# Second LayerNorm's turned tokens: stored from 128 partitions at a time, loaded back 32 partitions at a time

## The chip, the cores and the metric

One core of one Trainium2 chip. The metric is the device time of one execution in microseconds (us), lower is better; the time before is the median of three runs. A profiled execution gives, beside its own time, the span from the first to the last instruction of the program and the trace that the views below are taken from.

## The reference, cut to what matters

The input `x` has 2 batches of 2048 tokens of 512 features, in float32. A condition vector gives, through one matrix, six rows per batch (shift, scale and gate, twice).

```python
emb = dot(silu(t), ada_w) + ada_b            # six parts of 512
norm  = ln(x) * (1 + scale_msa) + shift_msa
h     = gelu(dot(norm, ssm_w1) + ssm_b1)
x     = x + gate_msa * (dot(h, ssm_w2) + ssm_b2)
norm2 = ln(x) * (1 + scale_mlp) + shift_mlp  # the second LayerNorm
hf    = gelu_tanh(dot(norm2, ff_w1) + ff_b1)
x     = x + gate_mlp * (dot(hf, ff_w2) + ff_b2)
```

## The kernel before

**Blocks.** The 4096 tokens are cut into eight blocks of 512 (`NBLK` = 8). A first part of the kernel runs `norm1(i)`, `ssm1(i)` and `ssm2(i)` for each block: the first LayerNorm and the two small products. Behind `ssm2(i)` comes `norm2(i)`, the second LayerNorm, whose result is kept in DRAM. A second part runs four steps `s` over pairs of blocks: `ff1(s)` for the pair, then `ff2(s, 0)` and `ff2(s, 1)`. The matrix products are cut by Winograd's variant of Strassen's scheme, so sums and differences of operands (lines 256 and 283) run on VectorE, GpSimd and ScalarE beside TensorE.

**Turning the tokens.** A product needs features on the partitions, LayerNorm has tokens there. `normed` (statistics, scales, then for each of four groups `c` of tokens a normalization on ScalarE and a transpose on VectorE, `turn`, line 591) does this in squares of 32 by 32. What comes out, the block `bl`, has partition `a*32 + q`, where `a` numbers a group of 32 partitions, and columns `(m, r)` with `m` of 4 and `r` of 512. The product needs it with `a` and `m` exchanged: partition `m*32 + q`, columns `(a, r)`. A DMA makes this exchange. There are three ways in the kernel:

- `move`: 16 DMAs of 64 KB from SBUF to SBUF, 32 partitions to 32 partitions. Only `norm1(2)` uses it.
- `turned_out`: four DMAs of 256 KB to DRAM, one for each `a`, each reading 32 partitions of `bl`, 8 KB from each, and writing pieces of 2 KB to the places where they belong in a DRAM tensor that has the wanted order. `norm1(3)` to `norm1(7)` use it, and one DMA of 1 MB (8 KB for each of 128 partitions) loads the whole block back. 
- `norm2(i)` uses the same `turned_out` for all eight blocks (`SOON` holds all of them). The blocks come back much later, in `normed2(i)` (called by `tokens(s)`, which `ff1(s)` calls): four DMAs of 256 KB, one for each `a`, each writing 2 KB to all 128 partitions.

After the loads `modulate` (ScalarE, line 274) applies scale and shift in place, one instruction for each of four feature groups `k`. Each reads all partitions and all `a`, so it needs all four loads. The pair's two token tiles `turned2[0]` and `turned2[1]` lie where the tokens of `norm1` lay before (`turned_r`): block 0 of the second part takes the place of `turned[6]`, block 1 that of `turned[7]`.

**Order.** `Plan` records every operation with a cost and the cells that it reads and writes, and `order()` simulates the engines to put all operations in one order. Each engine, and SyncE (SP) for nearly all DMAs, then runs its own in that order. A DMA's planned cost depends on its bytes. All DMAs are issued by line 316, all `tensor_tensor` work by line 256, all ScalarE activations by line 274, copies by line 283, matmuls by line 294. DMAs of SP rotate through eight semaphores; a DMA that takes a semaphore waits until the eighth DMA before it has landed.

**A reader's names.** In the views `far`, `ring`, `rows`, `near`, `hidden`, `fw` and `turned` are SBUF regions; `turned<-far` is a store of a turned block (norm1 and norm2 alike: `bl` lies in `far`, and the DRAM tensors too are called turned), `turned<-turned` a load back from DRAM.

Of the kernel before, what the change touches and what calls it, by code (L numbers as in the profile page):

```python
# [198 lines left out]
def kernel(  # L199
# [17 lines left out]
    P = 128  # L217
    B, N, D = x.shape
    H = fw1.shape[1]
    KD, KH = D // P, H // P  # L220
    C = 4
# [4 lines left out]
    G = 32  # L226
    SOON = tuple(range(NBLK))
# [14 lines left out]
    def cols(ap):  # L242
        n = 1
        for d in ap.shape[1:]:
            n *= d
        return n
# [64 lines left out]
    def dma(o, a, q="s", lead=0.0, lat=2000.0, sooner=0.0):  # L311
        size = max(cols(o.unsqueeze(0)), 1) * 4
        outs = [o] if o.tensor.name in scratch else []
        ins = [a] if a.tensor.name in scratch else []
        lead = lead or (0.0 if ins or not outs or size <= plan.LITTLE else 25000.0)
        plan.add(q, lambda E: E.dma_start(out=o, in_=a), outs, ins, {q: plan.ISSUE}, {q: lat}, size=size, lead=lead)  # L316
        plan.ops[-1].sooner = sooner
# [19 lines left out]
    def far(name, *shape):  # L337
        t = dram.tile(list(shape), F32, tag=name, name=name)
        scratch.add(t.tensor.name)
        return t  # L340

    def kb(t, at, n):
        return t[:, at * 256 : (at + n) * 256]

    def cut(t, form, **sizes):
        return t.rearrange(form, **sizes)
# [6 lines left out]
    for n in range(8):  # L353
        t = psum.tile([P, 2 * HT], F32, tag=f"bank{n}", name=f"bank{n}")
# [5 lines left out]

    x1_d = [far(f"x1_{i}", P, C, D) for i in range(NBLK)]
    turned1_d = {i: far(f"turned1_{i}", P, C, D) for i in range(3, NBLK)}
    turned_d = {i: far(f"turned_{i}", P, C, D) for i in SOON}
    fw1_d = far("fw1_parts", 7, P, 7, W)
    fw2_d = far("fw2_gated", P, KH, D)
    fw2_sd = far("fw2_sums", P, 3, KH // 2, D // 2)
# [4 lines left out]
    xs = [cut(slots[i % 5], "p (c d) -> p c d", c=C) for i in range(NBLK)]  # L371
# [15 lines left out]
    passing = (kb(near_r, 24, 2), kb(hidden_r, 30, 2))  # L387
# [128 lines left out]
    def stats(xt, slots=range(C)):  # L516
        t = marks[norms[0] % 4]
        norms[0] += 1
        mv = cut(t[:, :8], "p (c two) -> p c two", c=C)
        for c in slots:  # L520
            st, src, dst = t[:, 8 + 6 * c : 14 + 6 * c], xt[:, c, :], mv[:, c, :]
            plan.add("v", lambda E, st=st, src=src: E.bn_stats(st, src), [st], [src], {"v": 694}, {"v": 680})  # L522
            plan.add("v", lambda E, st=st, dst=dst: E.bn_aggr(dst, st), [dst], [st], {"v": 100}, {"v": 182})
        return t, mv

    STATS_BY_ACT = (2, 4, 5)
# [13 lines left out]
    def stats_by_act(xt, unread):  # L540

        t, mv = stats(xt, ())
        less, half = t[:, 52:56], D**-0.5
        for c in range(C):
            act_sum(unread, xt[:, c, :], AF.Identity, mv[:, c, :1], 0.0, 1.0 / D)
        small("g", lambda E: E.tensor_scalar(less, mv[:, :, 0], -half, None, ALU.mult), less, [mv[:, :, 0]])
        for c in range(C):
            act_sum(unread, xt[:, c, :], AF.Square, mv[:, c, 1:], less[:, c : c + 1], half)
        return t, mv

    def scales(t, mv, v="g", slots=slice(0, C)):
        full = [t[:, 32 + C * n : 32 + C * (n + 1)] for n in range(5)]
        ve, r, e, rstd, nmr = [a[:, slots] for a in full]
        var, mean, half = mv[:, slots, 1], mv[:, slots, 0], half_t[:, slots]
        small("g", lambda E: E.tensor_scalar(ve, var, 1.0, EPS, ALU.mult, ALU.add), ve, [var])
        small("g", lambda E: E.tensor_tensor(r, ve, half, ALU.pow), r, [ve, half], 1090)
        if v == "v":
            small(v, lambda E: E.tensor_tensor(e, r, ve, ALU.mult), e, [r, ve])
            small(v, lambda E: E.scalar_tensor_tensor(e, e, -0.5, r, ALU.mult, ALU.mult), e, [e, r])
            small(v, lambda E: E.scalar_tensor_tensor(rstd, e, 1.5, r, ALU.add, ALU.mult), rstd, [e, r])  # L560
            small(v, lambda E: E.scalar_tensor_tensor(nmr, mean, -1.0, rstd, ALU.mult, ALU.mult), nmr, [mean, rstd])
        else:
            small(v, lambda E: E.tensor_tensor(e, r, r, ALU.mult), e, [r])
            small(v, lambda E: E.tensor_tensor(e, e, ve, ALU.mult), e, [e, ve])
            small(v, lambda E: E.tensor_scalar(e, e, -0.5, 1.5, ALU.mult, ALU.add), e, [e])
            small(v, lambda E: E.tensor_tensor(rstd, r, e, ALU.mult), rstd, [r, e])
            small(v, lambda E: E.tensor_tensor(nmr, mean, rstd, ALU.mult), nmr, [mean, rstd])
            small(v, lambda E: E.tensor_scalar(nmr, nmr, -1.0, None, ALU.mult), nmr, [nmr])
        return full[3], full[4]
# [4 lines left out]
    def normal(o, xt, c, rstd, nmr, e="a"):  # L574
        dst, src, b, s = slot(o, c), xt[:, c, :], nmr[:, c : c + 1], rstd[:, c : c + 1]
        if e == "a":
            act(dst, src, AF.Identity, b, s)
        else:
            plan.add(
                "v",  # L580
                lambda E: E.tensor_scalar(dst, src, s, b, ALU.mult, ALU.add),
                [dst],
                [src, b, s],
                {"v": 560},
                {"v": 640},
            )

    def turn(bl, src, c):
        o = cut(bl, "p (m k c q) -> p k m c q", m=C, k=KD, c=C)[:, :, :, c, :]
        a = cut(slot(src, c), "p (k m q) -> p k m q", k=KD, m=C)  # L590
        plan.add("v", lambda E: E.transpose(o, a), [o], [a], {"v": 636}, {"v": 705})  # L591

    def modulate(t, k, which, b):
        o = t[:, :, k * P : (k + 1) * P]
        act(o, o, AF.Identity, mods[which][:, k, b : b + 1], mods[which + 1][:, k, b : b + 1])
# [3 lines left out]
    def next_blocks():  # L599
        turns[0] += 1  # L600
        return blocks[turns[0] % 2]
# [9 lines left out]
    def normed(src, dst, bl, by_act=False):  # L611
        t, mv = stats_by_act(src, banks[2]) if by_act else stats(src)
        rstd, nmr = scales(t, mv)
        for c in range(C):
            normal(dst, src, c, rstd, nmr)
            turn(bl, dst, c)
        return cut(bl, "p (m r) -> p m r", m=C)

    def move(to, bl, queues="s"):
        for a in range(C):  # L620
            for m in range(C):
                q = queues[m % len(queues)]
                dma(to[m * G : (m + 1) * G, a, :], bl[a * G : (a + 1) * G, m, :], q, lat=2000.0 + 16 * plan.ISSUE / len(queues))

    def turned_out(to, bl):
        for a in range(C):
            dma(to[:, a].rearrange("(m q) r -> q m r", m=C), bl[a * G : (a + 1) * G])
# [50 lines left out]

    def norm2(i):
        plan.stage = f"norm2 {i}"  # L680
        turned_out(turned_d[i], normed(xs[i], passing if i else xs[i], next_blocks(), i in STATS_BY_ACT))

# [317 lines left out]
    def normed2(i):  # L1002
        plan.stage = f"tokens {i}"
        t = turned2[i % 2]
        if i in SOON:
            for a in range(C):
                dma(t[:, a], turned_d[i][:, a])
        else:
            dma(t, x1_d[i])
            move(t, normed(t, t, kb(far_r, 0, 8)))  # L1010
        for k in range(KD):
            modulate(t, k, 3, i // PER_B)

    def tokens(s):
        plan.stage = f"tokens {s}"
        q = {}
        for n in range(2):
            i = 2 * s + n
            if i in SOON:
                normed2(i)  # L1020
            q[f"1{n + 1}"], q[f"2{n + 1}"] = turned2[n][:, :, :W], turned2[n][:, :, W:]
        return second(q, thirds(outer_s), cuts=2)
# [381 lines left out]
    modulation(3, 1)  # L1404
    plan.care = 0.3
    norm2(0)
    load_ada(5)
    modulation(4, 2)
# [8 lines left out]
    for i in range(1, NBLK):  # L1417
        if i + 3 < NBLK:
            plan.care = 0.2
            tok[i + 3] = norm1(i + 3)  # L1420
            plan.care = 0.45
        last = i + 2 >= NBLK
        hooks = second_head(i + 1, hid[i + 1]) if last and i + 1 < NBLK else {}
        ssm2(i, hid[i], w2_ops, CARRIED, hooks)
        if i in SOON:
            norm2(i)
        if i == 4:
            ff = weight_fw2(0, 1)
            fw2_sixth(*ff)
        if i + 1 == PER_B:  # L1430
            w2_ops = weight2(1, 1)
            quarter_row(1)
            w2_leaves[0] = second_leaves(w2_ops)
        if not last:
            hid[i + 2] = ssm1(i + 2, tok[i + 2], w1_ops, second_head(i + 1, hid[i + 1]))
# [62 lines left out]
```

## Time and profile before

| what | value |
|---|---|
| median of three runs | 568.1 us (567.44 to 570.17) |
| profiled execution, its own time | 569.21 us |
| its span, first to last instruction | 567.4 us |
| granted TensorE clock | 0.999 |
| moved by DMA | 119.85 MB, mean 211 GB/s |

The span is what the views divide up; 1.8 us of the profiled execution's own time lie outside it. PE is TensorE's matmuls, PEld its weight loads, DVE VectorE, ACT ScalarE, POOL GpSimd, SPq the issues on SyncE's queue. In the timeline a row merges neighbours of one kind: start, duration from the first start to the last end, and the count.

### The profile page before, as it was taken

The page shows a single profiled execution, that of the slowest core. Times are in us where ns is not written, and L with a number is a line of the kernel's source. Part 1 is how long each engine was busy: PE and PEld are TensorE (multiplying, and loading weights), DVE is VectorE, ACT ScalarE, POOL GpSimd, SP SyncE. Part 2 cuts the span into 40 slices and gives each one's busy share as a digit, 9 for nine tenths or more (in the row PEclk, how much of TensorE's full clock was granted, in tenths as well). Part 3 has the DMA queues.
Part 4 walks back from the last instruction along what each step waited for, and adds up shares of the span by engine and source line. Part 5 has one row for each costly group of instructions (what it writes and reads, how often), then busy time and mean ns, then how long its engine had stood idle before and what let it go on. Part 6 is the DMA issues. An engine that isn't in the chain of part 4 may idle for free.

```text
span 567.4 us, 10428 instructions
## 1 busy us (share of the span) xinstructions
PE 559.0 (99%) x3577; PEld 506.5 (89%) x3577; DVE 489.0 (86%) x918; ACT 271.8 (48%) x558; POOL 384.1 (68%) x523
## 2 busy tenths in 40 slices
PE   8999999899999999999999999999999999999997
PEld 4888889788897988889999889999889999888997
DVE  5696988799886988989989889999999898789785
ACT  3464856777685875659112356222266222335120
POOL 2887547598934598994767897667795685446660
PEclk9999999999999999999999999999999999999999
DMA  8954899987899867896054889168955041820022
GB/s 314 399 217 90 246 360 277 320 299 264 258 310 307 270 217 220 276 317 217 20 186 152 304 279 342 68 205 274 319 174 207 2 150 43 273 93 29 1 75 74
DMA packets 53057, 119.85 MB, mean 211 GB/s; under 512 B 5473, under 2 KB 10509, under 8 KB 51470
## 3 DMA queue, kind: packets, MB, share of 16 engines
q1 hardware_dynamic: 51842, 118.66, 62.6%
q8 instruction: 28, 0.46, 0.4%
q10 hardware_dynamic: 1164, 0.55, 0.3%
q14 instruction: 23, 0.19, 0.1%
HBM read 77.63 MB, written 40.51 MB: 208 GB/s over the span
## 4 chain that ended last, share of the span: by engine, by line
PE 89%; DMA 6%; DVE 2%; ACT 1%; SPq 1%; issue 0%; DVEq 0%; ACTq 0%
PE bank L294 89%; DMA turned<-turned 3%; DMA turned<-far 2%; DMA fw<-in_L_cond_ada_w_dram 1%; SPq L316 1%; DVE far L591 1%; PE bank L304 0%; DVE rows L256 0%; ACT hidden L274 0%; ACT turned L274 0%; ACT near L274 0%; DVE marks L522 0%; ACT bank L283 0%; DVE ring L256 0%; DVE turned L656 0%
## 5 line engine op out<-in xcount | busy, mean ns | idle before, releaser
L294 PE MATMUL bank<-turned,ring 128*128 128x256 f32 x896 | 209.1, 380 | 1.2 <-ACT turned L274 1.0
L294 PEld LDWEIGHTS bank<-turned,ring 128*128 128x128 f32 x896 | 167.3, 190 | 24.8 <-ACT turned L274 1.8
L256 DVE TENSOR_TENSOR hidden<-bank,hidden 128x512 f32<-128x512 f32 (+1 forms) x171 | 124.8, 755 | 26.9 <-PE bank L294 23.5
L294 PE MATMUL bank<-near,hidden 128*128 128x256 f32 (+1 forms) x470 | 95.6, 350 | 1.8 <-DVE rows L256 1.8
L294 PEld LDWEIGHTS bank<-near,hidden 128*128 128x128 f32 x470 | 82.1, 190 | 11.8 <-DVE rows L256 2.6
L294 PE MATMUL bank<-fw,hidden 128*128 128x128 f32 x640 | 91.0, 276 | 0.0
L256 DVE TENSOR_TENSOR rows<-bank,rows 128x128 f32<-128x128 f32 (+3 forms) x154 | 78.8, 555 | 9.4 <-PE bank L294 8.8
L294 PE MATMUL bank<-ring 128*128 128x256 f32 x336 | 82.5, 381 | 0.0
L294 PEld LDWEIGHTS bank<-fw,hidden 128*128 128x128 f32 x640 | 81.3, 192 | 0.5
L283 ACT COPY bank<-bank 128x512 f32<-128x512 f32 (+2 forms) x88 | 37.2, 424 | 78.0 <-PE bank L294 77.2
L294 PEld LDWEIGHTS bank<-ring 128*128 128x128 f32 x336 | 63.2, 190 | 10.9 <-issue 2.1
L256 POOL TENSOR_TENSOR turned<-turned 128x512 f32<-128x512 f32 (+1 forms) x58 | 63.8, 1114 | 13.2 <-ACT turned L274 6.7
L294 PE MATMUL bank<-fw,far 128*128 128x128 f32 (+1 forms) x656 | 67.4, 275 | 0.1
L256 POOL TENSOR_TENSOR hidden<-hidden 128x128 f32<-128x128 f32 (+2 forms) x52 | 45.6, 881 | 28.8 <-DVE hidden L256 13.5
L274 ACT ACTIVATE hidden<-hidden,cols 128x512 f32<-128x512 f32 (+1 forms) x66 | 44.9, 711 | 38.4 <-DVE hidden L256 38.3
L294 PEld LDWEIGHTS bank<-fw,far 128*128 128x128 f32 (+1 forms) x656 | 61.2, 168 | 1.7 <-issue 1.3
L294 PE MATMUL bank<-fw,near 128*128 128x128 f32 x464 | 61.0, 275 | 0.0
L294 PEld LDWEIGHTS bank<-fw,near 128*128 128x128 f32 x464 | 56.4, 192 | 0.0
L256 POOL TENSOR_TENSOR fw<-fw 128x256 f32<-128x256 f32 (+1 forms) x51 | 42.0, 838 | 14.8 <-DVE turned L256 7.9
L274 ACT ACTIVATE turned<-turned,mod,mod 128x512 f32<-128x512 f32 x56 | 41.9, 805 | 15.5 <-DMA turned<-turned 14.8
L256 DVE TENSOR_TENSOR hidden<-hidden 128x512 f32<-128x512 f32 (+2 forms) x58 | 37.7, 665 | 1.9 <-POOL hidden L256 1.3
L256 POOL TENSOR_TENSOR ring<-turned,ring 128x256 f32<-128x256 f32 x40 | 29.7, 752 | 12.4 <-PE bank L294 6.4
(141 smaller groups left out, 710.2 us busy)
## 6 DMA issues: line engine op xcount, KB each, us to landing
ring<-fw_parts SPq DMA_DIRECT2D x28, 512.0 KB
turned<-far SPq DMA_DIRECT2D x52, 256.0 KB
ring<-fw_parts SPq DMA_DIRECT2D x28, 384.0 KB
rows<-x SPq DMA_DIRECT2D x32, 256.0 KB
turned<-turned SPq DMA_DIRECT2D x32, 256.0 KB
out_dram<-rows SPq DMA_DIRECT2D x28, 256.0 KB
fw_parts<-fw SPq DMA_DIRECT2D x21, 256.0 KB
fw<-in_L_cond_ada_w_dram SPq DMA_DIRECT2D x5, 1024.0 KB
```

The source lines that it names most:

```text
L256: lambda E: E.tensor_tensor(o, a, b, f),
L274: lambda E: E.activation(o, a, func, bias=bias, scale=scale),
L283: plan.add("a", lambda E: E.copy(o, a), [o], [a], {"a": cost}, {"a": cost + 60})
L294: lambda E: E.matmul(o, lhsT, rhs, start=start, stop=stop, skip_group_check=True, **kw),
L316: plan.add(q, lambda E: E.dma_start(out=o, in_=a), outs, ins, {q: plan.ISSUE}, {q: lat}, size=size, lead=lead)
L591: plan.add("v", lambda E: E.transpose(o, a), [o], [a], {"v": 636}, {"v": 705})
```

## The change

The DRAM tensor of each block gets the order `(m, 128 partitions, r)`, which is the order of `bl` itself. A store now takes one `m` of all 128 partitions (2 KB of each) and writes 256 KB that lie together in DRAM. The exchange of `a` and `m` moves to the load: each load fills one group of 32 partitions with 8 KB each, gathered from four pieces of 2 KB that lie 64 KB apart. Number and bytes of the DMAs stay: four stores and four loads of 256 KB for each block. `norm1` keeps `turned_out`.

```diff
-    turned_d = {i: far(f"turned_{i}", P, C, D) for i in SOON}
+    turned_d = {i: far(f"turned_{i}", C, P, D) for i in SOON}
...
     def norm2(i):
         plan.stage = f"norm2 {i}"
-        turned_out(turned_d[i], normed(xs[i], passing if i else xs[i], next_blocks(), i in STATS_BY_ACT))
+        bl = normed(xs[i], passing if i else xs[i], next_blocks(), i in STATS_BY_ACT)
+        for m in range(C):
+            dma(turned_d[i][m], bl[:, m, :])
...
         if i in SOON:
-            for a in range(C):
-                dma(t[:, a], turned_d[i][:, a])
+            for m in range(C):
+                dma(t[m * G : (m + 1) * G], turned_d[i][m].rearrange("(a q) r -> q a r", a=C))
```

## The prediction

> **What bounds the kernel now.** I read the page first, then who made TensorE wait, then the chain that ended last, then SP's queue and the DMA rates around the places that the chain names.
>
> ```profile
> span 567.4 us, 10428 instructions
> PE 559.0 (99%) x3577; PEld 506.5 (89%) x3577; DVE 489.0 (86%) x918; ACT 271.8 (48%) x558; POOL 384.1 (68%) x523
> ...
> turned<-far SPq DMA_DIRECT2D x52, 256.0 KB
> ...
> turned<-turned SPq DMA_DIRECT2D x32, 256.0 KB
> ```
>
> TensorE is busy for 559.0 of 567.4 us. The change touches no TensorE instruction, so it can act only through the waits that TensorE has, or through a new one. Of the 52 stores of 256 KB, 32 are norm2's and change shape; 20 are those of norm1(3) to norm1(7) and stay. The 32 loads of 256 KB all change.
>
> The waits of TensorE, summed by what ended them (total us, times, longest):
>
> ```profile
> PE bank L294 <- DVE rows L256: 1.8, 2, 1.5
> PE bank L294 <- POOL small L321: 1.3, 1, 1.3
> PE bank L294 <- ACT turned L274: 1.0, 1, 1.0
> PE bank L294 <- DVE turned L656: 0.2, 1, 0.2
> ```
>
> Two of them (L321, L656) belong to the start, before any turned block exists. What is left is 1.8 + 1.0 = 2.8 us in three places. That is a ceiling for any gain: 0.5% of 568.1, about what a measurement of this kernel can tell from no change, is 2.84 us. Now the chain of work, in order of time (start, duration, what):
>
> ```profile
> 86.64 0.33 SPq L316
> ...
> 88.22 5.22 DMA turned<-far
> ...
> 93.52 8.61 DMA turned<-turned
> ...
> 163.03 0.71 DVE far L591
> ...
> 165.74 5.57 DMA turned<-far
> ...
> 171.36 7.94 DMA turned<-turned
> ...
> 179.33 0.82 ACT turned L274
> ...
> 180.19 0.70 PE bank L294 x2
> ```
>
> Twice the chain leaves TensorE for a DMA round trip, and both are norm1's: four stores and, after the last has landed, the load of 1 MB. The second is norm1(7): last transpose at 163.03, last store issued at 165.74 and landed at 171.31, load from 171.36 to 179.30, modulation, TensorE at 180.19 after its wait of 1.0. None of these DMAs is changed, but they share the queue with changed ones:
>
> ```profile
> 43.17 10.79 SPq L316 DMA_DIRECT2D turned<-far  x16
> ...
> 86.64 2.82 SPq L316 DMA_DIRECT2D turned<-far  x4
> ...
> 131.79 2.39 SPq L316 DMA_DIRECT2D turned<-far  x4
> ...
> 153.85 3.11 SPq L316 DMA_DIRECT2D turned<-far  x4
> ...
> 160.92 1.99 SPq L316 DMA_DIRECT2D fw<-in_L_cond_ff_w_dram  x2
> 163.77 3.33 SPq L316 DMA_DIRECT2D turned<-far  x4
> 168.00 4.16 SPq L316 DMA_DIRECT2D turned<-turned  x5
> ...
> 193.39 2.12 SPq L316 DMA_DIRECT2D turned<-turned  x4
> ...
> 202.23 2.80 SPq L316 DMA_DIRECT2D turned<-far  x4
> ```
>
> By the kernel's order the stores at 153.85 are norm2(3)'s, those at 163.77 norm1(7)'s. The five loads from 168.00 are the 1 MB of norm1(7), issued at 171.36 by the chain, and the four of block 0 for the second part. Of these, three go ahead of it, as the DMA view of a stretch before 171.36 lists:
>
> ```profile
> turned<-turned SPq DMA_DIRECT2D x3, 256.0 KB
> ```
>
> So the one place where a changed load stands before critical work is here. At the other DMA round trip (86.64 to 102.13) no changed transfer lies between store and load.
>
> **The change part by part.** It removes and adds no instruction: four stores and four loads for each block, 256 KB each, before and after. Bytes, and which store and readers each load depends on, stay as they are in the planner's account, so I expect the same order of instructions on every engine. Only the shapes of 64 transfers differ. The price is therefore the time of a 2 KB piece, since every one of these DMAs is cut into 128 pieces of 2 KB, eight for each of 16 DMA engines. From a stretch's DMA share and GB/s, the last two columns, the time of 2 KB on one engine is 16 x 2048 x share / (GB/s) in ns:
>
> ```profile
> 45.00:52.00 7.00, 7.00 (x34) 6.17 (x33) 4.00 (x14) 2.33 (x6) 6.68 (x20) 1.00 0.42 103
> 138.00:140.50 2.50, 2.50 (x17) 2.29 (x17) 2.50 (x7) 2.50 (x7) 2.12 (x2) 1.00 1.07 415
> 163.00:164.00 1.00, 1.00 (x10) 1.00 (x9) 0.90 (x2) 1.00 (x4) 0.34 (x1) 1.00 0.46 150
> 168.30:170.30 2.00, 2.00 (x13) 1.82 (x12) 2.00 (x4) 1.86 (x5) 0.69 (x1) 1.00 0.87 273
> 204.00:206.50 2.50, 2.50 (x18) 2.29 (x17) 2.30 (x4) 1.80 (x4) 2.15 (x8) 1.00 0.98 236
> 260.90:263.40 2.50, 2.50 (x24) 2.50 (x24) 2.50 (x6) 2.50 (x7) 0.00 (x0) 1.00 0.96 339
> ```
>
> - Stores from 32 partitions in a quiet queue (204.00, those issued at 202.23): 32768 x 0.98 / 236 = 136 ns.
> - Loads into 128 partitions in a quiet queue (260.90, those of a block of the second part): 32768 x 0.96 / 339 = 93 ns.
> - Stores from 32 partitions behind a longer queue: 84 ns (138.00, after those of 131.79) and 104 ns (168.30, mostly norm1(7)'s stores).
> - Writing 32 partitions: the 16 moves of norm1(2) from 43.17 do it, from SBUF to SBUF, 134 ns (45.00). So the write side in quiet looks like the read side.
>
> A 32-partition transfer thus costs 136 - 93 = 43 ns more per piece in a quiet queue, 0.34 us per DMA, and between -9 and 11 ns more behind a queue, -0.07 to 0.09 us per DMA. [...]
>
> [...]
>
> *Loads.* Ahead of norm1(7)'s load stand three changed loads. Value: 3 x 0.09 = 0.3 us, from the row at 168.30, which is this place and this queue. Ends: 3 x (-0.07) = -0.2 and 3 x 0.34 = 1.0 us. It is paid in full if at all: ACT waits for this load, TensorE for ACT. The 64 KB steps in DRAM of the new loads are shown by no row; norm2's stores step further (8 KB and 256 KB in DRAM) and show the 136 ns at most.
>
> *Stores.* Removed from norm2(3)'s four stores is up to 4 x 0.34 us of transfer and the pressure on SP's issue. What norm1(7) can get of it is bounded by its stores in a quiet queue, those at 86.64: four issues in 2.82 us instead of 3.33, last landing 5.22 after its issue instead of 5.57. So at most 0.51 + 0.35 = 0.86 us, and at least nothing, because the DMA engines had nearly drained (share 0.46 at 163.00) when norm1(7)'s stores began. I take a third, 0.3 us. The other seven blocks' stores have loads much later and no chain row behind them: 0; should SP be what holds something back there, they too would only give time.
>
> *Other loads.* Four 32-partition DMAs take at most 88.22 + 5.22 - 86.64 = 6.8 us from first issue to last landing in a quiet queue and 165.74 + 5.57 - 163.77 = 7.5 us in a full one. What hides that is the time to the modulation, here the tightest blocks:
>
> ```profile
> 406.27 1.37 SPq L316 DMA_DIRECT2D turned<-turned  x3
> ...
> 431.85 1.74 SPq L316 DMA_DIRECT2D turned<-turned  x4
> ```
>
> ```profile
> 200.54 4.33 ACT L274 ACTIVATE turned<-turned,mod,mod 128x512 f32<-128x512 f32 x6
> ...
> 414.98 0.81 ACT L274 ACTIVATE turned<-turned,mod,mod 128x512 f32<-128x512 f32 x1
> ...
> 439.52 1.51 ACT L274 ACTIVATE turned<-turned,mod,mod 128x512 f32<-128x512 f32 x2
> ```
>
> Block 7: 431.85 + 6.8 = 438.7 against 439.52. Block 6: 406.27 + 7.5 = 413.8 against 414.98. Block 1: 193.39 + 7.5 = 200.9; the modulations from 200.54 start with two of block 0 as I read the due times, so block 1's first is at about 201.9. All still fit, with 0.8 us or more to spare. If the cover goes, ACT waits in order, and the copies and GELUs queued behind the modulation wait with it, TensorE next. Behind the loads on SP stand weight loads for `ff1`.
>
> Sum: 0.3 - 0.3 + 0 = 0.0 us. Against the profiled execution, whose span is 567.4 and own time 569.21, that is 569.2; that execution was 1.1 us above the median of the three runs, so the forecast on the median's scale is 568.1.
>
> **Rivals.**
>
> *A, slower:* the new loads crowd on one group of partitions even in the queue. For it speaks that the three start right behind norm1(7)'s stores, which have the same habit, and that the pieces take 136 and 134 ns in quiet on both sides; against it the 84 ns at 138.00. Price: 1.0 us at 180.19 and no relief from the stores, 569.1. It decides from about 120 ns per piece in 170 to 174 us. To pass 2.84 us the loads would have to be worse than any row here, 8 x 3 pieces of over 210 ns: 571.0 and up. [...]
>
> *B, faster:* the stores' relief comes whole and the loads cost nothing: -0.86 - 0.2, 567.0. For it: SP issues almost without a pause from 153.85 to 163, so its time is tight there. Against it: the drained engines at 163.00. It cannot pass 2.8 us, the ceiling above.
>
> *C, the change does not do what it says:* the 136 ns come from the scattered places in DRAM and not from the partitions, and the new loads, scattered in DRAM too, show 93 ns or 136 just the same. Then norm1's and norm2's rows change little: 568.1 to 569.1.
>
> **How the numbers follow.** Forecast (within 0.5 us of 568.1) 0.45, A at its price 0.22, A beyond 0.5% or ACT waits that I have missed 0.15, B 0.10, C 0.05, faster by over 0.5% through something that no view shows 0.03. Within 0.5%: 0.45 + 0.22 + 0.10 + 0.05 = 0.82; slower 0.15; faster 0.03. The likeliest is 568.1. The range goes from B's 567.0 to 570.5, which takes in A and part of what lies beyond it; the three runs before spread over 567.44 to 570.17 by themselves.
>
> **What would show it.** Instructions in the same order on all engines. Norm2's stores in quiet (near 204) at about 93 ns per piece instead of 136, the four issues in about 1.8 us instead of 2.80. Loads of a block in quiet (near 260) at 136 instead of 93. TensorE's wait for turned tokens at about 180 us: 1.0 in the forecast, 2.0 in A, near zero in B. No new ACT wait for turned tokens near 202, 415 and 439. The prediction is wrong if TensorE waits at the start of an `ff1` step, or if norm1(7)'s load takes over 9 us from issue to landing.

## The result and the profile after

| | before | changed |
|---|---|---|
| median of 13 runs each | 568.49 us | 571.42 us |
| lowest to highest | 566.80 to 570.26 | 569.13 to 576.62 |
| profiled execution: own time, span | 569.21, 567.4 us | 576.62, 574.8 us |

The ratio is 1.0049, 95% interval 1.0031 to 1.0068: slower by 2.8 us, just inside the 0.5% that the prediction called no change, and above the end of its range, 570.5. The profiled execution is the slowest of the 13. Its places can be read, but its sum is more than the change typically costs, so each size below is also taken from a timed comparison.

The instructions stand in the same order on TensorE, VectorE, ScalarE and GpSimd. On SP one store and one load of `rows` have changed places. The page of the changed kernel:

```profile
span 574.8 us, 10427 instructions
PE 562.5 (98%) x3577; PEld 508.3 (88%) x3577; DVE 489.0 (85%) x918; ACT 272.0 (47%) x558; POOL 381.9 (66%) x523
...
PEclk9999999999999999999999999999979999999999
```

Of 7.4 us more span, 562.5 - 559.0 = 3.5 are longer TensorE work and 12.3 - 8.4 = 3.9 are more idle time. The first is not more matmuls (3577 as before): the 30th slice of the clock row shows a 7. Who made TensorE wait (total us, times, longest):

```profile
PE bank L294 <- DVE hidden L256: 3.0, 1, 3.0
PE bank L294 <- DVE rows L256: 2.1, 4, 0.8
PE bank L294 <- POOL small L321: 1.3, 1, 1.3
PE bank L294 <- ACT turned L274: 0.7, 1, 0.7
```

The wait for `turned` at norm1(7), on which the prediction spent its sum, went from 1.0 to 0.7. The 3.0 for `hidden` is new. The chain of the changed kernel around it (start, duration, what):

```profile
408.19 12.28 DMA turned<-turned
...
420.66 0.81 ACT turned L274
421.47 0.52 ACT hidden L283
...
422.01 0.70 DVE hidden L256
...
422.75 1.65 PE bank L294 x3
```

Read it backwards: TensorE waits for a VectorE sum, that for a ScalarE copy, that stands in ScalarE's queue behind a modulation, and the modulation waits for the last of block 6's loads, 12.28 us from issue to landing. ScalarE's timeline of the changed kernel (start, duration, what, in brackets the idle time before it and who ended it):

```profile
415.44 0.62 ACT L283 COPY hidden<-hidden 128x512 f32<-128x512 f32 x1 [0.32 <-DVE hidden L256]
420.66 0.81 ACT L274 ACTIVATE turned<-turned,mod,mod 128x512 f32<-128x512 f32 x1 [4.60 <-DMA turned<-turned]
421.38 0.60 ACT L283 COPY hidden<-hidden 128x512 f32<-128x512 f32 x1
```

Before, the same modulation ran at 414.98 without a pause. Block 6's modulated tokens are used only by the next step, `ff1(3)`; it is the copy behind the modulation that TensorE needs now. Block 5 shows the same in small, a wait of 1.67 at 356.25 where before none was; through GpSimd's and VectorE's sums it reached TensorE at 367.64:

```profile
356.25 3.64 ACT L274 ACTIVATE turned<-turned,mod,mod 128x512 f32<-128x512 f32 x5 [1.67 <-DMA turned<-turned]
```

```profile
367.64 0.71 PE L294 MATMUL bank<-fw,hidden 128*128 128x128 f32 x4 [0.83 <-DVE rows L256]
```

ScalarE also waits 1.24 for block 1's tokens at 202.19 and 1.75 for block 7's at 448.60, where before it did not; behind these two TensorE has no new wait of over 0.4.

The rates, by the prediction's formula (last two columns: DMA share and GB/s), of the changed kernel:

```profile
204.00:206.20 2.20, 2.20 (x15) 2.04 (x15) 2.13 (x5) 2.20 (x4) 1.26 (x5) 1.00 0.60 236
261.00:265.00 4.00, 4.00 (x39) 4.00 (x38) 4.00 (x9) 3.32 (x11) 0.73 (x1) 1.00 1.06 230
408.00:416.00 8.00, 8.00 (x39) 7.04 (x38) 7.47 (x14) 3.88 (x7) 6.54 (x9) 1.00 1.05 213
```

Stores in quiet take 32768 x 0.60 / 236 = 83 ns per 2 KB, loads in quiet 32768 x 1.06 / 230 = 151 ns. The third row is block 6's loads in a queue that holds weight loads too, so it is a mean over both: 32768 x 1.05 / 213 = 162 ns. The same stretch of the kernel before gives 32768 x 0.76 / 271 = 92 ns:

```profile
408.00:416.00 8.00, 8.00 (x39) 7.04 (x38) 7.32 (x13) 3.42 (x6) 6.70 (x7) 1.00 0.76 271
```

### The profile page after: what moved, and what is told of

The parts are those of the page before. It is cut to its first block, busy times and chain, and to the rows that moved or that the text cites. A ratio compares the mean times of both kernels' runs of the same rounds, so it can differ in the third digit from the quotient of the medians.

```text
span 574.8 us, 10427 instructions
## 1 busy us (share of the span) xinstructions
PE 562.5 (98%) x3577; PEld 508.3 (88%) x3577; DVE 489.0 (85%) x918; ACT 272.0 (47%) x558; POOL 381.9 (66%) x523
## 4 chain that ended last, share of the span: by engine, by line
PE 77%; DMA 10%; POOL 5%; DVE 3%; ACT 2%; issue 1%; SPq 1%; DVEq 0%; ACTq 0%; POOLq 0%
PE bank L294 76%; DMA turned<-turned 5%; DMA turned<-far 2%; DMA fw<-in_L_cond_ada_w_dram 1%; SPq L316 1%; DMA fw_sums<-rows 1%; DVE hidden L256 1%; ACT turned L274 1%; POOL far L256 1%; POOL ring L256 1%; DVE rows L256 1%; POOL turned L256 1%; POOL rows L256 1%; ACT hidden L274 1%; DVE far L591 1%
## 5 line engine op out<-in xcount | busy, mean ns | idle before, releaser
L294 PE MATMUL bank<-ring 128*128 128x256 f32 x336 | 83.8, 385 | 0.4 <-DVE rows L256 0.3
L256 DVE TENSOR_TENSOR hidden<-hidden 128x512 f32<-128x512 f32 (+2 forms) x58 | 39.4, 694 | 1.9 <-POOL hidden L256 1.3
```

What stands on the lines that cost most here:

```text
L256: lambda E: E.tensor_tensor(o, a, b, f),
L294: lambda E: E.matmul(o, lhsT, rhs, start=start, stop=stop, skip_group_check=True, **kw),
```

## The experiments

The theory after the result, H (the first expectations call it P): loads that write 32 neighbouring partitions are slow also behind other transfers; a modulation on ScalarE therefore waits, and what stands behind it in ScalarE's order, needed much sooner, waits with it. The rivals, with letters of their own, not those of the prediction: N, the loss lies at norm1(7), where three changed loads go ahead of its load; D, it is the 64 KB steps in DRAM; B, slower loads delay the weight loads that share the queue, and TensorE waits for weights. The table has every kernel beside the kernel before on the same chip, five rounds each.

| kernel | us | before | ratio, 95% interval |
|---|---|---|---|
| e1 new stores alone | 568.22 | 569.43 | 0.9987 (0.9977 to 0.9998) |
| e2 new loads alone | 571.78 | 569.43 | 1.0050 (1.0033 to 1.0066) |
| e3 both, blocks 0 to 3 | 568.98 | 569.43 | 0.9988 (0.9971 to 1.0004) |
| e4 both, blocks 4 to 7 | 572.81 | 569.43 | 1.0059 (1.0033 to 1.0086) |
| e5 new stores, DRAM rows far apart | 567.49 | 569.23 | 0.9973 (0.9955 to 0.9990) |
| e6 changed, loads in another order | 571.13 | 568.64 | 1.0037 (1.0023 to 1.0051) |
| e7 changed, modulations held back | 568.84 | 569.23 | 0.9996 (0.9979 to 1.0013) |
| e8 before, modulations held back | 568.60 | 569.23 | 0.9991 (0.9977 to 1.0005) |
| e9 loads of every fourth partition | 568.03 | 569.23 | 0.9975 (0.9961 to 0.9990) |
| e10 one load of 1 MB | 571.52 | 568.64 | 1.0045 (1.0031 to 1.0059) |

### Stores alone, loads alone

e1 keeps the changed stores and loads 2 KB into all 128 partitions; the exchange of `a` and `m` is left out, so it computes something else:

```diff
-                dma(t[m * G : (m + 1) * G], turned_d[i][m].rearrange("(a q) r -> q a r", a=C))
+                dma(t[:, m], turned_d[i][m])
```

> The new store (128 partitions, 256 KB together in DRAM) with loads of 128 partitions, 2 KB each, of the same tensor: the exchange of a and m is left out, so the tokens come in a wrong order. Theory P (loads that write 32 partitions run at about half rate behind a queue, come late for ScalarE, and TensorE waits): no such loads here, so no wait for turned tokens near 356, 420 and 448, loads at 84 to 95 ns per 2 KB, and the stores' relief alone is left: 0.5 to 1 us below the kernel before, ratio 0.998 to 0.999. Rival S (the new stores cost something): ratio near the changed kernel's 1.005. Rival D (the 64 KB steps in DRAM of the new loads are slow, not the partitions) expects the same as P here.

e2 keeps the stores of before and loads 32 neighbouring partitions, 8 KB each, one piece of DRAM without steps:

```diff
-            for a in range(C):
-                dma(t[:, a], turned_d[i][:, a])
+            for m in range(C):
+                dma(t[m * G : (m + 1) * G], turned_d[i][m * G : (m + 1) * G])
```

> The store and the DRAM order of the kernel before, and loads that write 32 partitions, each a stretch of 256 KB that lies together in DRAM, 8 KB for each partition. Theory P: the loads are as slow as the changed kernel's (over 150 ns per 2 KB in the stretch 408 to 416), ScalarE waits for them near 420, ratio 1.004 to 1.008, a little above the changed kernel since the stores' relief is missing. Rival D: without the steps in DRAM the loads run at 84 to 95 ns per 2 KB and the ratio is 1.000. Rival S: 1.000.

The stores gain 0.7 us (0.9987), the loads lose 2.8 (1.0050): the loss is the loads'. The window of block 6 gives e1 32768 x 0.84 / 289 = 95 ns, and e2 32768 x 1.03 / 258 = 131 ns, slow but under the 150 that was expected:

```profile
408.00:416.00 8.00, 8.00 (x39) 7.04 (x38) 7.24 (x12) 3.46 (x6) 6.70 (x7) 1.00 0.84 289
```

```profile
408.00:416.00 8.00, 8.00 (x39) 7.04 (x38) 7.78 (x14) 3.71 (x7) 6.54 (x10) 1.00 1.03 258
```

In e2's profile ScalarE waits for block 6's tokens, but only 1.66 us, and no TensorE wait follows at 420:

```profile
419.15 0.81 ACT L274 ACTIVATE turned<-turned,mod,mod 128x512 f32<-128x512 f32 x1 [1.66 <-DMA turned<-turned]
```

At the place of block 5 TensorE waits in e2 exactly as long as in the changed kernel:

```profile
369.09 0.71 PE L294 MATMUL bank<-fw,hidden 128*128 128x128 f32 x4 [0.83 <-DVE rows L256]
```

This wait, 0.82 or 0.83 us, stands in the profiles of all four kernels that load 32 neighbours for blocks 5 and 6 and have the modulations in their old place (changed, e2, e4, e6), and in no profile of the others. At block 6 the wait varies: 2.96 in the changed kernel, 1.94 in e4, 1.09 in e6, none in e2. The rest of e2's loss is not found in its one profile; a wait of 1.5 us at its start, for a DMA of a bias, is not it, for e5 has 2.2 there and is faster than the kernel before.

### Which blocks

e3 and e4 use the changed form for half of the blocks and that of before for the rest (`NEW = (0, 1, 2, 3)` or `(4, 5, 6, 7)`):

```diff
+        if i not in NEW:
+            turned_out(turned_d[i], bl)
+            return
...
+                if i not in NEW:
+                    dma(t[:, m], turned_d[i][:, m])
+                    continue
```

> The new form for blocks 0 to 3 alone, the old for 4 to 7. Theory P: the loads of blocks 2 and 3 have time, those of 5, 6 and 7 are the old ones again, so no wait of ScalarE near 356 and 420; the stores' relief at norm1(4) and norm1(7) stays: ratio 0.998 to 1.000. Rival N (the loss is at norm1(7), behind the loads of block 0): near 1.005, since these loads are still here.

> The new form for blocks 4 to 7 alone. Theory P: the late loads of blocks 5 and 6 are here and the relief of the early stores is not: ScalarE waits near 356 and 420, ratio 1.005 to 1.008. Rival N: 1.000.

Blocks 0 to 3, which hold the loads ahead of norm1(7), lose nothing: -0.7 us, interval -1.7 to 0.2. N falls. Blocks 4 to 7 lose 0.0059 x 569.43 = 3.4 us. The halves add up to 2.7, the whole change's 2.8, though with intervals this wide the agreement is no proof. In e4's waits the same wait for `hidden` stands at block 6, and beside it 0.7 us for a weight load, which B would have:

```profile
PE bank L294 <- DVE hidden L256: 1.9, 1, 1.9
...
PE bank L294 <- DMA ring<-fw_parts: 0.7, 1, 0.7
```

### The steps in DRAM

e5 stores from and loads into all 128 partitions, with rows of 2 KB that lie 64 KB apart in DRAM; the exchange is left out again:

```diff
-    turned_d = {i: far(f"turned_{i}", C, P, D) for i in SOON}
+    turned_d = {i: far(f"turned_{i}", P, 32, D) for i in SOON}
...
-            dma(turned_d[i][m], bl[:, m, :])
+            dma(turned_d[i][:, m], bl[:, m, :])
...
-                dma(t[m * G : (m + 1) * G], turned_d[i][m].rearrange("(a q) r -> q a r", a=C))
+                dma(t[:, m], turned_d[i][:, m])
```

> Stores from and loads into 128 partitions, 2 KB each, but every row of 2 KB lies 64 KB from the next in DRAM (the exchange is left out). Theory P (the partitions written make the new loads slow): about the stores-alone kernel, ratio 0.998 to 1.000, and 84 to 95 ns per 2 KB between 405 and 421 us. Rival D (64 KB steps in DRAM are slow): over 120 ns there, ScalarE waits near 420, ratio 1.003 or more.

The ratio is 0.9973, a little below the range expected, and block 6's loads take 32768 x 0.75 / 272 = 90 ns. With 128 partitions the steps cost nothing, and e2's loads are slow without them; D falls.

```profile
408.00:416.00 8.00, 8.00 (x38) 7.04 (x38) 7.34 (x12) 2.79 (x5) 7.15 (x8) 1.00 0.75 272
```

### Loads as slow, but nothing queued behind the wait

e7 is the changed kernel with the modulations of blocks 4 to 7 put later in ScalarE's order; e8, its control, does the same to the kernel before. With the number the planner does not start the operation earlier than 15 us of its simulated time before it is due:

```diff
+            plan.ops[-1].lead = 15000.0 if i >= 4 else 0.0
```

> The changed kernel, with the modulations of blocks 4 to 7 held back in the planned order until 15 us before they are due; loads and their rates as changed. Theory H (the loss is ScalarE's: a modulation that waits for a late load holds the copies and GELUs behind it, and TensorE waits for these): no TensorE wait of over 0.5 us near 367 and 419, ratio at most 0.001 above its control, near 0.999 to 1.001. Rival B (the slow loads take bandwidth from the weights of ff1, and these come late): the loss stays, ratio 1.004 or more above the control.

> The control for the run before: the kernel before with the same modulations held back. No load is late in it, so both theories expect a ratio of 0.998 to 1.002; what differs from 1 is the price of the other order.

e7 takes 0.9996 of the kernel before, its control 0.9991: with the modulations held back the change costs 0.0005, 0.3 us, of 2.8. By the two intervals (0.0005 + 0.0022 at the most) up to about 1.5 us of cost would still fit. The loads are still slow: 32768 x 1.04 / 263 = 130 ns at block 6, as in e2 if not the 162 of the changed kernel. From the issue of the first of block 5's last three loads to the landing of the last, by the semaphores in the traces, 10.4 us pass in e7, 10.2 in the changed kernel and 6.7 before. Yet the waits at 367 and 422 are gone, and weight loads share the queue as in the changed kernel. So B cannot be the main cause, and H holds: the slow loads cost time mostly through what ScalarE has queued behind them. The window and TensorE's waits of e7 (the 0.7 for `rows` is at 104.82, before any changed load):

```profile
408.00:416.00 8.00, 8.00 (x39) 7.04 (x38) 7.52 (x12) 1.72 (x3) 6.74 (x8) 1.00 1.04 263
```

```profile
PE bank L294 <- DVE rows L256: 0.9, 2, 0.7
...
PE bank L294 <- DVE hidden L256: 0.3, 1, 0.3
```

### Fewer partitions, or neighbours

e9 has the stores of before, and four loads that each fill 32 partitions with 8 KB as in e2, but every fourth partition instead of neighbours:

```diff
-            for a in range(C):
-                dma(t[:, a], turned_d[i][:, a])
+            for m in range(C):
...
+                to, src = t[m::C], turned_d[i][m::C]
```

> As the kernel with the old store and loads of 32 partitions with 8 KB each, but each load takes every fourth partition (0, 4, 8 ... then 1, 5, 9 ...) in place of 32 neighbours. [...] Rival: it is the number of partitions of one DMA, wherever they lie: as slow as that kernel, ratio 1.004 to 1.006.

The planner's account still names the neighbours, so the order is that of e2. The ratio is 0.9975 (0.9961 to 0.9990) where neighbours gave 1.0050. e9 computes the whole reference and is faster than the changed kernel and than the kernel before, which it undercuts by 1.4 us. In e9 block 6's last three loads are issued from 403.91; the stretch around them gives 32768 x 0.90 / 301 = 98 ns, and the modulation starts without a pause:

```profile
403.00:411.00 8.00, 8.00 (x39) 7.04 (x38) 7.80 (x14) 3.63 (x7) 6.54 (x10) 1.00 0.90 301
```

```profile
412.62 0.81 ACT L274 ACTIVATE turned<-turned,mod,mod 128x512 f32<-128x512 f32 x1
```

Two measures that need no window say the same. Block 6's four loads are 128 packets of 8 KB in e2 and in e9, the only ones of that size around them: 538 ns each on average in e2, 350 in e9, or 135 and 88 ns per 2 KB. And from the first issue of block 6's last three loads to the last landing 6.8 us pass before and 6.9 in e9, but 10.3 in e2, 10.0 in e7 and 13.2 in the changed kernel.

So it is not that a load fills 32 partitions, it is which 32 (131 ns for neighbours, 98 for every fourth). Why that is so, no run shows. Why e9 is faster than the kernel before is not shown: its packets are also larger (8 KB in place of 2 KB), and no run separates the two.

### The order of the four loads

e6 is the changed kernel with its loads in the order m = 0, 2, 1, 3:

```diff
-            for m in range(C):
+            for m in (0, 2, 1, 3):
```

> The changed kernel with the four loads of a block issued in the order m = 0, 2, 1, 3, so that loads that follow each other fill partitions 0 to 31, 64 to 95, 32 to 63, 96 to 127. [...]

The window at block 6 gives 32768 x 1.03 / 265 = 127 ns instead of 162, and the wait for `hidden` is 1.1. But e7, with the loads in the order of the changed kernel, has 130 there too, and e6's last three loads take 12.0 us from first issue to last landing, between e7's 10.0 and the changed kernel's 13.2. In the time, 1.0037 (1.0023 to 1.0051) overlaps the changed kernel's interval, so whether the order gains anything is not settled.

```profile
408.00:416.00 8.00, 7.64 (x36) 6.42 (x35) 6.97 (x14) 3.35 (x7) 6.54 (x8) 1.00 1.03 265
```

### One load for a block

e10 is the kernel before with one load of 1 MB for each block in place of four:

```diff
-            for a in range(C):
-                dma(t[:, a], turned_d[i][:, a])
+            dma(t, turned_d[i])
```

> The kernel before with one load of 1 MB for each block of the second part in place of four of 256 KB: 128 partitions, 8 KB for each, as norm1 has it. The planned order differs in the second part. Theory P: full rate and fewer issues, like the loads of every fourth partition, ratio 0.996 to 1.000. If the quarter loads matter because ScalarE or SP gets its pieces earlier, 1.000 to 1.003.

This expectation was missed: the ratio is 1.0045. Its loads are not slow, 32768 x 0.86 / 284 = 99 ns at block 6 where the kernel before has 92, so it is another loss. Its profile shows TensorE waiting 2.03 for norm1(7)'s tokens, ahead of whose load the whole of block 0 now stands, and a mean granted clock of 0.76 over the 7 us behind that wait. The clock is not the cause: the five executions beside the profiled one have a mean granted clock of 1.000 and take 570.60 to 572.05. But with fewer DMAs the planned order changes too, and that was not taken apart. Its cause stays open.

```profile
408.00:416.00 8.00, 8.00 (x39) 7.05 (x38) 7.14 (x14) 3.17 (x5) 7.25 (x9) 1.00 0.86 284
```

```profile
180.66 5.68 PE L294 MATMUL bank<-turned,ring 128*128 128x256 f32 x16 [2.03 <-ACT turned L274]
```

## Why the prediction was wrong

*Order and counts.* This was right: the same order on the four compute engines, and as many DMAs.

*Stores.* This was right in kind: 83 ns per piece in quiet where 93 was forecast and 136 stood before, four issues in 1.94 us where 1.8 was forecast:

```profile
201.28 1.94 SPq L316 DMA_DIRECT2D turned<-far  x4
```

They were put at 0.3 us of relief with 0.86 as the end; e1 measured 0.7 (0.1 to 1.3).

*Loads ahead of norm1(7).* Nothing contradicts the size. Its load took 8.47 us from issue to landing, 0.53 more than before, where 0.3 was forecast and 1.0 was the end; TensorE's wait there still fell to 0.7, since the last store was issued 0.77 sooner and took 4.69 instead of 5.57. But single executions do not resolve tenths here: this wait is 1.4 in e3's profile and none in e6's, with changed loads at this place, and 1.0 before and none in e8's, with the old ones. By the time, e3 loses nothing. The chain of the changed kernel:

```profile
164.97 4.69 DMA turned<-far
...
169.72 8.47 DMA turned<-turned
```

*Other loads: the step that failed.* It said that "four 32-partition DMAs take at most" 6.8 us in quiet and 7.5 in a full queue, and "all still fit, with 0.8 us or more to spare". Both bounds came from stores, which read 32 partitions. In the changed kernel the first of block 6's last three loads was issued at 407.25 and the last landed at 408.19 + 12.28 = 420.47: 13.2 us against 7.5, and e2 and e7, each in one execution, have 10.3 and 10.0. What the rows at 138.00 and 168.30 showed for reading (84 and 104 ns behind a queue) does not hold for writing (162 ns). Block 5, whose wait reached TensorE in four profiles, was not among the blocks looked at. The term was put at 0 and measured 2.8 us for the loads alone (e2, 1.9 to 3.8), 3.4 with the changed stores in blocks 4 to 7 (e4, 1.9 to 4.9).

The sentence after it, what happens "if the cover goes", had the path right: ACT waits in order, the copies wait with it, TensorE next. e7 against e8 (0.3 us left of 2.8, at most about 1.5) shows that most of the loss takes it. The watched signs, new waits of ACT near 202, 415 and 439, all came: 1.24 us at 202.19, 4.60 at 420.66 and 1.75 at 448.60. Loads of a block in quiet were forecast at 136 ns and took 151. The two signs that were to prove the prediction wrong did not come: norm1(7)'s load stayed under 9 us, and TensorE's new waits lie inside steps, not at the start of one. That the ratio is still inside 0.5% is luck: nothing in the prediction's sum kept it there.

*Rivals of the prediction.* A had the right transfers, loads that are slow behind other transfers too (162 ns against 92 at block 6), but the wrong place: it was priced at norm1(7), where three loads cost little, and at block 6 by no row at all. The 0.15 for ACT waits that were missed is where the result lies. Of B one half came, the stores' relief (0.7 us of its 0.86), but the loads were not free. C did not come: the stores' pieces fell to 83 ns, and e2, e5 and e9 together (131, 90 and 98 ns) show that with the loads it is the partitions and not DRAM.

Why reading 32 neighbours behind a queue costs little (84 and 104 ns, against 93 for loads into 128 partitions in quiet) where writing costs much (162 in the changed kernel, 131 in e2), no run here settles.

## What to carry to other kernels

A transfer's time from one direction, or from a calm stretch, is no bound for the other direction behind a busy queue (7.5 us forecast from stores, 13.2 measured for loads); have a row for the very case or price the cover as if it were lost. An operation that isn't due before the next step can still cost time at once, if on an engine that works in order something needed soon stands behind it (4.60 us of ScalarE's wait for block 6, 2.96 of TensorE's): check the cover against its place in that order, not against its use. Where a load must fill few partitions, try them spread out (every fourth of 128 here) and not next to one another (98 against 131 ns per 2 KB); shown here for loads of 32 partitions with 8 KB each.

## What was not expected of the hardware

The wait of 2.96 us was followed by seven microseconds at half the granted clock (column before the last two):

```profile
422.00:429.00 7.00, 6.25 (x15) 4.99 (x16) 4.50 (x6) 3.41 (x6) 2.19 (x3) 0.51 0.11 42
429.00:436.00 7.00, 7.00 (x34) 6.17 (x33) 6.29 (x7) 3.78 (x7) 4.73 (x6) 1.00 0.38 131
```

So in this execution the wait cost its 3 us about twice: the 3.5 us of longer TensorE work on the page are this stretch. e4's wait of 1.94 us was followed by a clock of 1.00, e10's of 2.03 by a mean of 0.76 over the next 7 us (the two rows below).

The mean granted clock of every execution is on record. Seven microseconds at half clock lower it by 7 x 0.49 / 575 = 0.006, and the profiled execution has 0.994; the other twelve of the changed kernel have 0.999 or 1.000. So the 2.8 us that the change typically costs are lost without such a stretch. In e4 five of the twelve executions have 0.997 and take 573.14 to 575.89 us, seven have 1.000 and take 568.21 to 573.48, with a median of 571.65: part of e4's 3.4 us is probably clock.

```profile
423.00:430.00 7.00, 7.00 (x33) 6.17 (x34) 6.80 (x9) 5.30 (x10) 3.98 (x5) 1.00 0.27 90
```

```profile
180.00:187.00 7.00, 6.33 (x24) 5.07 (x25) 4.93 (x8) 5.32 (x11) 2.10 (x3) 0.76 0.65 259
```
